# The states' products of a linear-attention layer: from two row groups and two PSUM banks to four of each

## The chip, the cores and the metric

One core of one Trainium2 chip runs the whole program. The metric is the device time of one execution in microseconds (us). The kernel before took 1279.37 us, the median of three runs (1279.18 to 1280.09).

## What is computed

The input is 8 sequences of 256 tokens with 256 features. They are normalised, and two branches read the result: an attention with 16 heads and 64 states to each head, and a feed-forward part with 4-bit weights (width 2048). Both are added to the input. The part that the change touches is `s` below and what is made of it.

```
xn = layernorm(x)
q, k = rope(xn @ Wq.T), rope(xn @ Wk.T)          # 16 heads of 128
v, g = xn @ Wv.T, xn @ Wg.T
s   = clip(xn @ Ws1.T @ Ws2.T + bs2, -32, 32)    # rank 16; 16 heads of 64 states
z   = cumlogsumexp(s, over the tokens)
es, enz = exp(s), exp(-z)
A   = tril(q @ k.T * scale)
ok  = enz * (A @ es)
qv  = softmax(ok, over the states)
W2  = tril((qv * enz) @ es.T)
o   = W2 @ v
o_g = o * rsqrt(mean(o * o) + 1e-5) * g_norm_weight * (g * sigmoid(g))
x + o_g @ Wo.T + ((gelu(xn @ Wg4.T) * (xn @ Wu4.T)) @ Wd4.T)
```

All arithmetic is in float32. The exponential of `s` is needed in two layouts: `es` with tokens on the partitions, `esT` with states on the partitions. `enz` is made from `esT` by a running sum along the tokens and a reciprocal.

## The kernel before

**Steps.** The 2048 tokens are cut into 4 groups of 512 (`G`, two sequences each), the 16 heads into 8 pairs. A step `n` is one group and one pair of heads, so there are 32 steps. Each works in three overlapping stretches: in the round of the main loop before its own the products of its states (`states`, L390) and of its rotated queries and keys (`rope`, L428); in its own round values and gates (`vg`, L482), scores (L500), logits (L517) and softmax (L540); in the next round the rest (`turn`, `weights`, `outputs`, `turn_back`, `close`). The feed-forward part (`ffn`, L344) is fed between them piece by piece, and so is the decoding of its 4-bit weights on VectorE (`decode_next`, L231).

**Order.** The order is fixed when the program is built. Tables (`POS`, `START`, `FEED`, L33 to L52) give every piece a place within its round; the main loop (L684) sorts them, calls each in turn, and after each call runs `tick` (L97). A piece issues its matmuls at once and leaves the work of the other engines behind as a chain (a Python generator); each `tick` issues one stage of every chain. So TensorE's instructions stand in the order of the pieces, and the other engines' in the order in which stages come up. On every engine the instructions then run in that order, and semaphores hold each back until its operands are there.

**Banks.** All products go to PSUM tiles of one bank (128 x 512 float32), from a pool of 8 (`bank`, L122). `new` (L103) makes a ninth user wait at build time: `need` (L92) ticks until the chains that read the eighth-last tile have been issued. On the chip, the first matmul into a bank waits for the last read of its former tenant.

**The low-rank input.** Once a group, `low_rank` (L373) multiplies the normalised tokens by `w_s1`. The 16 columns of `Ws1` stand twice among its 64 columns, at 0 and at 32, so the product `ps[0:64]` has the 16 values of each token on rows 0 to 15 and again on rows 32 to 47. ScalarE copies it to `rT` (L385) with a bias that is 1 on rows 16 and 48, so that the row of `bs2` in `w_s2` is added by the product itself. `w_s2` has the 17 rows at 0 and at 32 as well; it is loaded by four transfers on SyncE's queue (L167 to L169), after `w_s1` (L165) and `one_at` (L166) and ahead of the first attention weights (L170).

**The states.** In each call of `states`, 4 matmuls (L401) have a token block of `rT[0:17]` as the stationary operand and write `ps` (tokens on partitions), and 4 (L402) have the weights' 17 rows at 32 as the stationary operand and write `psT` (states on partitions). They alternate. VectorE then clamps both banks (L412, 512 elements each, `esT` first), ScalarE takes the exponentials (L415), VectorE the running sums (L420) and the reciprocals (L426).

**Around it.** In most rounds the logits (L526, read by L535), the weights of the step before (L596 and L600, read and masked by L497) and the states follow each other on TensorE, and then the transposes of the softmax (L547), which read the result of L535.

Of the kernel before, what the change touches and what calls it, by code (L numbers as in the profile page):

```python
# [10 lines left out]
F32 = mybir.dt.float32  # L11
I32 = mybir.dt.int32
AF = mybir.ActivationFunctionType
ALU = mybir.AluOpType
# [3 lines left out]
P = 128  # L18
B, T, D = 8, 256, 256
H, DK, M = 16, 128, 64  # L20
MLP = 2048
NTOK = B * T
G = 512
NG = NTOK // G
TC = G // P
EPS = 1e-5
CLAMP = 32.0
# [33 lines left out]
def layer_kernel(ctx: ExitStack, tc: tile.TileContext, a: dict, out: bass.AP):  # L61
# [15 lines left out]
    nc = tc.nc  # L77

    const = ctx.enter_context(tc.tile_pool(name="const", bufs=1))
# [5 lines left out]
    p1 = ctx.enter_context(tc.tile_pool(name="p1", bufs=1))  # L85
# [6 lines left out]
    def need(*gens):  # L92

        while any(c in chains for c in gens):
            tick()
# [7 lines left out]
    def new(pool, shape, tag, bufs=1, dtype=F32):  # L103

        users = held.setdefault(tag, [])
        if len(users) >= bufs:
            need(*users[-bufs])
        t = pool.tile(shape, dtype, tag=tag, name=tag, bufs=bufs)
        users.append([])
        at_tag[id(t)] = t, users[-1]  # L110
        return t
# [3 lines left out]
    def chain(gen, *tiles):  # L115

        chains.append(gen)
        for t in tiles:
            at_tag[id(t)][1].append(gen)
        return gen  # L120

    def bank():  # L122
        return new(ps_p, [P, 512], "ps", 8)
# [3 lines left out]
    xT = const.tile([P, 2, NTOK], F32, tag="xT", name="xT")  # L127
# [5 lines left out]
    cos = const.tile([P, T], F32, tag="cos", name="cos")  # L133
    sin = const.tile([P, T], F32, tag="sin", name="sin")

    w_s1 = const.tile([P, 2, 64], F32, tag="w_s1", name="w_s1")
    w_s2 = const.tile([64, H * M], F32, tag="w_s2", name="w_s2")
    one_at = const.tile([64, 1], F32, tag="one_at", name="one_at")
    gw = const.tile([P, 1], F32, tag="gw", name="gw")
    w_o = const.tile([P, H, D], F32, tag="w_o", name="w_o")  # L140
    w_gate = const.tile([P, 2, MLP], F32, tag="w_gate", name="w_gate")
# [14 lines left out]
    def load_w(n, k):  # L156

        if n < N:
            w = aw.tile([P, 2, 2, 2 * DK], F32, tag=f"wts{k}", name=f"wts{k}")
            nc.sync.dma_start(out=w, in_=a["wqkvg"][steps[n][1]][:, k : k + 2])  # L160
            wts[n, k] = w
# [2 lines left out]
    load_x(2, 2)  # L164
    nc.sync.dma_start(out=w_s1.rearrange("p c f -> p (c f)"), in_=a["ws1"])  # L165
    nc.sync.dma_start(out=one_at, in_=a["one_at"])  # L166
    for r in (0, 32):  # L167
        nc.sync.dma_start(out=w_s2[r : r + 16, :], in_=a["ws2"])
        nc.sync.dma_start(out=w_s2[r + 16 : r + 17, :], in_=a["bs2"])  # L169
    load_w(0, 0)  # L170
    nc.sync.dma_start(out=cos, in_=a["cos"])
    nc.sync.dma_start(out=sin, in_=a["sin"])
# [200 lines left out]
    def low_rank(g):  # L373

        need(*normed[g])
        rT = p1.tile([64, G], F32, tag="rT", name="rT")
        ps = bank()
        for c in range(2):
            nc.tensor.matmul(
                ps[0:64, :], lhsT=w_s1[:, c, :], rhs=xT[:, c, g * G : (g + 1) * G],  # L380
                start=c == 0, stop=c == 1,
            )

        def work():
            nc.scalar.activation(rT, ps[0:64, :], AF.Identity, bias=one_at)  # L385
            yield

        rTs[g] = rT, chain(work(), ps)

    def states(n):  # L390

        g, hp = steps[n]
        ms = slice(hp * P, (hp + 1) * P)
        (rT, c), to = rTs[g], of[n]
        need(c)
        es = to["es"] = new(p1, [P, TC, P], "es")
        esT = to["esT"] = new(p2, [P, G], "esT", 2)
        ps, psT = bank(), bank()
        for i in range(TC):
            ts = slice(i * P, (i + 1) * P)  # L400
            nc.tensor.matmul(ps[:, ts], lhsT=rT[0:17, ts], rhs=w_s2[0:17, ms], start=True, stop=True)  # L401
            nc.tensor.matmul(  # L402
                psT[:, ts], lhsT=w_s2[32:49, ms], rhs=rT[32:49, ts], start=True, stop=True
            )


        enz = to["enz"] = new(p2, [P, G], "enz", 2)

        def work():
            both = ((esT, psT), (es.rearrange("p i m -> p (i m)"), ps))  # L410
            for t, q in both:
                nc.vector.tensor_scalar(t, q, CLAMP, -CLAMP, ALU.min, ALU.max)  # L412
            yield
            for t, q in both:
                nc.scalar.activation(t, t, AF.Exp)  # L415
            yield
            for b in range(2):
                e = esT[:, b * T : (b + 1) * T]

                nc.vector.tensor_tensor_scan(  # L420
                    enz[:, b * T : (b + 1) * T], e, e, 0.0, ALU.add, ALU.max
                )
            yield
            for i in range(TC):
                r = enz[:, i * P : (i + 1) * P]
                nc.vector.reciprocal(r, r)  # L426
                yield

        to["states"] = chain(work(), ps, psT, es, esT, enz)

    def rope(n, j, which):

# [251 lines left out]
    for n in range(-1, N + 1):  # L684
        at = []
# [14 lines left out]
        if n == -1:  # L700
            put_norm(0, [0.0] * 4 + [0.1] * 2)
            put_at(0.2, low_rank, 0)
        if n + 1 < N:
            if n >= 0 and steps[n][1] == 7:
                put("low", 0, low_rank, steps[n][0] + 1)
            put("states", 0, states, n + 1)
            for k, (j, which) in enumerate(((0, 0), (0, 1), (1, 0), (1, 1))):
                put("rope", k, rope, n + 1, j, which)
            put("rope", 3, load_w, n + 2, 0)
# [45 lines left out]
def _tables():  # L755

    pos = np.arange(T, dtype=np.float32)
    inv = np.float32(1.0) / np.float32(10000.0) ** (
        np.arange(0, DK, 2, dtype=np.float32) / np.float32(DK)
    )  # L760
    ang = (pos[None, :] * inv[:, None].astype(np.float32)).astype(np.float32)
    c, s = np.cos(ang).astype(np.float32), np.sin(ang).astype(np.float32)
    return np.concatenate([c, c]), np.concatenate([-s, s])


def _layout(x):

    c = np.ascontiguousarray
    half = MLP // 2

    def pairs(ws):
        w = np.stack([w.T.reshape(P, 2, H // 2, 2 * DK) for w in ws])
        return c(w.transpose(3, 1, 0, 2, 4))

    def packed_in(w):
        return c(w.reshape(half, 2, -1).transpose(2, 1, 0).reshape(-1, MLP))

    def quarters(spread, of):
        ws = [packed_in(n[ff + w + of]).reshape(-1, 2, 4, 256) for w in ("gate", "up")]
        ws = [w.transpose(2, 0, 1, 3).reshape(4, -1, 512) for w in ws]  # L780
        w = n[ff + "down" + of]
        w = w.T.reshape(8, -1, D).transpose(1, 0, 2).reshape(-1, 4, 512)
        ws.append(w.transpose(1, 0, 2))
        return c(np.stack([[spread(w[q]) for w in ws] for q in range(4)]).reshape(12, P, 512))

    cos, sin = _tables()
    n = {k: np.asarray(v) for k, v in x.items()}
    at, ff = "L0_attn_", "L0_ffn_"
    return {
        "x": c(n[at + "hidden_states"].reshape(NTOK, D)),  # L790
        "wqkvg": pairs([n[at + w] for w in ("Wq", "Wk", "Wv", "Wg")]),
        "wo": c(n[at + "Wo"].T.reshape(H, DK, D).transpose(1, 0, 2)),
        "ws1": c(np.pad(n[at + "Ws1"].T.reshape(P, 2, 1, 16), [(0, 0)] * 3 + [(0, 16)]).repeat(2, 2).reshape(P, 128)),
        "one_at": (np.arange(64) % 32 == 16).astype(np.float32).reshape(64, 1),
        "ws2": c(n[at + "Ws2"].T),
        "bs2": c(n[at + "bs2"].reshape(1, H * M)),
        "gw": c(n[at + "g_norm_weight"].reshape(DK, 1)),
        "codes": quarters(lambda w: w, "_W_packed"),
        "scales": quarters(lambda w: w.repeat(16, 0), "_scales"),
        "cos": c(cos),  # L800
        "sin": c(sin),
    }
# [17 lines left out]
```

## Time and profile before

| | us |
|---|---|
| median of three runs | 1279.37 |
| the profiled execution, whole | 1279.47 |
| its span, first to last instruction | 1277.6 |
| L401 and L402, TensorE busy, each | 36.9 |
| L412 (`esT` and `es`), VectorE busy | 21.9 and 21.8 |
| L379, TensorE busy | 9.3 |
| L497, VectorE busy | 129.2 |

The profile is one execution. Engines are PE (TensorE's matmuls), PEld (TensorE's loads of the stationary operand), DVE (VectorE), ACT (ScalarE), POOL (GpSimd) and SP (SyncE, which issues the DMAs). A row of groups has the source line, the engine and the operation, tiles written and read, shapes, the number of records, then busy time in us and the mean of one in ns, then the idle time of the engine just before them. A matmul's shape "17*128" is 17 contracted rows by 128 columns of the stationary operand. A row of the timeline has start, duration (both us), engine, line, operation, tiles, shape, count, and in brackets how long the engine was idle before and what released it. The chain that ended last is followed back from the last instruction, at each step to what released it. Busy time counts overlapping records of one line once in some views and a group's mean is over single records, so the two need not multiply out.

### The profile page before, as it was taken

To read this page: it belongs to the slowest core of one execution; us is meant where nothing else is said; L and a number is where in the kernel's file an instruction comes from. 1 tells how busy PE (TensorE), PEld (TensorE's weight loads), DVE (VectorE), ACT (ScalarE), POOL (GpSimd) and SP (SyncE) were. 2 spreads that over 40 slices of the span, in tenths; PEclk is the share of its full clock that TensorE was granted. 3 is DMA by queue.
4 is the path that set the end of the run, shared out by engine and by line. 5 is a ranking of instruction groups with operands and counts; after the bars stand their busy time and mean duration, and the time that the engine had idled before them with its cause. 6 is when DMAs were issued, how large, how long until landed. Compare 5 with 4: busy or idle time off the path is not lost.

```text
span 1277.6 us, 17557 instructions
## 1 busy us (share of the span) xinstructions
PE 1262.4 (99%) x6448; PEld 914.2 (72%) x6448; DVE 817.4 (64%) x1592; ACT 531.9 (42%) x1677; POOL 441.9 (35%) x408
## 2 busy tenths in 40 slices
PE   7999999999999999999999999999999999999998
PEld 4577777776777777767677687777777767777776
DVE  6968756666656576664665766756665566566444
ACT  2444443453433454352444424445343345434232
POOL 4434333443223443232433413444332344322311
PEclk9999999999999999999999999999999999999999
DMA  4301111110111110011110010101001111101000
GB/s 162 116 17 50 34 33 50 34 49 2 50 34 34 50 33 18 17 34 50 50 34 17 31 38 33 34 33 34 1 33 34 34 33 32 36 17 43 25 17 17
DMA packets 18361, 47.73 MB, mean 37 GB/s; under 512 B 1986, under 2 KB 6466, under 8 KB 18276
## 3 DMA queue, kind: packets, MB, share of 16 engines
q1 hardware_dynamic: 18276, 46.61, 11.1%
q8 instruction: 51, 0.84, 0.3%
q14 instruction: 34, 0.28, 0.1%
HBM read 44.51 MB, written 2.10 MB: 36 GB/s over the span
## 4 chain that ended last, share of the span: by engine, by line
PE 94%; DVE 4%; ACT 1%; issue 1%; POOL 0%; DMA 0%; POOLq 0%; DVEq 0%; ACTq 0%
PE ps L489 16%; PE ps L437 16%; PE ps L669 9%; PE ps L338 8%; PE ps L318 8%; PE ps L298 8%; PE ps L507 4%; PE ps L526 4%; PE ps L596 3%; PE ps L401 2%; PE ps L621 2%; PE ps L618 2%; PE ps L617 2%; PE ps L510 2%; PE ps L651 2%; PE ps L547 1%
## 5 line engine op out<-in xcount | busy, mean ns | idle before, releaser
L450 POOL TENSOR_TENSOR z<-z,sin 128x512 f32<-128x512 f32 x128 | 163.3, 1276 | 448.8 <-ACT z L447 448.5
L437 PE MATMUL ps<-xT,wts 128*128 128x512 f32 x512 | 240.9, 593 | 0.0
L489 PE MATMUL ps<-wts,xT 128*128 128x256 f32 x1024 | 239.7, 379 | 0.0
L489 PEld LDWEIGHTS ps<-wts,xT 128*128 128x128 f32 x1024 | 191.9, 190 | 55.8 <-issue 30.8
L437 PEld LDWEIGHTS ps<-xT,wts 128*128 128x128 f32 x512 | 94.3, 191 | 85.1 <-issue 79.3
L497 DVE TENSOR_TENSOR at<-ps,mask 128x384 f32<-128x384 f32 x256 | 129.2, 551 | 21.6 <-PE ps L510 9.4
L306 POOL TENSOR_SCALAR t<-t 128x512 f32<-128x512 f32 x64 | 40.1, 627 | 267.0 <-ACT t L304 265.0
L446 ACT COPY z<-ps 64x512 f32<-64x512 f32 x128 | 74.6, 583 | 135.9 <-PE ps L437 117.5
L415 ACT ACTIVATE esT<-esT 128x512 f32<-128x512 f32 x32 | 20.2, 630 | 252.4 <-DVE esT L412 252.4
L298 PE MATMUL ps<-xT,w_gate 128*128 128x512 f32 x256 | 120.7, 594 | 0.0
L318 PE MATMUL ps<-xT,w_up 128*128 128x512 f32 x256 | 120.6, 593 | 0.0
L277 DVE TENSOR_TENSOR res<-ps,res 128x512 f32<-128x512 f32 x64 | 44.1, 689 | 119.5 <-PE ps L338 59.8
L338 PE MATMUL ps<-w_down,inter 128*128 128x256 f32 x512 | 116.0, 380 | 0.9 <-DVE inter L326 0.9
L426 DVE RECIPROCAL enz<-enz 128x128 f32<-128x128 f32 x128 | 116.8, 932 | 0.0
L669 PE MATMUL ps<-w_o,ogT 128*128 128x256 f32 x512 | 115.6, 379 | 0.0
L338 PEld LDWEIGHTS ps<-w_down,inter 128*128 128x128 f32 x512 | 95.9, 190 | 14.4 <-DVE inter L326 1.7
L669 PEld LDWEIGHTS ps<-w_o,ogT 128*128 128x128 f32 x512 | 95.6, 190 | 14.6 <-issue 2.2
L448 DVE TENSOR_TENSOR k<-ps,cos 128x512 f32<-128x512 f32 x64 | 44.0, 687 | 87.2 <-ACT z L447 87.1
L451 POOL TENSOR_TENSOR q<-q,z 128x512 f32<-128x512 f32 x64 | 81.6, 1275 | 21.7 <-DVE q L448 13.9
L451 POOL TENSOR_TENSOR k<-k,z 128x512 f32<-128x512 f32 x64 | 81.5, 1273 | 9.0 <-DVE k L448 4.3
L448 DVE TENSOR_TENSOR q<-ps,cos 128x512 f32<-128x512 f32 x64 | 44.0, 688 | 63.0 <-ACT z L447 62.7
L559 ACT ACTIVATE pr<-ps,mx 128x64 f32<-128x64 f32 x256 | 76.5, 325 | 12.9 <-DVE mx L556 12.3
(81 smaller groups left out, 2119.5 us busy)
## 6 DMA issues: line engine op xcount, KB each, us to landing
wts<-in_wqkvg_dram SPq DMA_DIRECT2D x64, 512.0 KB, 3.6
pk<-in_codes_dram SPq DMA_DIRECT2D x12, 256.0 KB, 4.5
sc<-in_scales_dram SPq DMA_DIRECT2D x12, 256.0 KB, 4.7
w_o<-in_wo_dram SPq DMA_DIRECT2D x4, 512.0 KB, 6.0
out_dram<-res SPq DMA_DIRECT2D x8, 256.0 KB, 2.1
res<-in_x_dram SPq DMA_DIRECT2D x3, 512.0 KB, 5.4
res<-in_x_dram SPq DMA_DIRECT2D x2, 256.0 KB, 2.8
w_s<-in_ws_dram SPq DMA_DIRECT2D x3, 64.0 KB, 2.4
```

The lines of the kernel that those rows point to most:

```text
L298: nc.tensor.matmul(pg, lhsT=w_gate[:, c, ns], rhs=xT[:, c, gs], start=c == 0, stop=c == 1)
L318: nc.tensor.matmul(pu, lhsT=w_up[:, c, ns], rhs=xT[:, c, gs], start=c == 0, stop=c == 1)
L338: nc.tensor.matmul(ps[:, k, :], lhsT=inter[g, n][0][:, (i + k) * P : (i + k + 1) * P], rhs=w_dn[:, n, :], start=n == 2 * q, stop=n == 2 * ...
L426: nc.vector.reciprocal(r, r)
L437: nc.tensor.matmul(ps, lhsT=w[:, c, :], rhs=xT[:, c, g * G : (g + 1) * G], start=c == 0, stop=c == 1)
L448: nc.vector.tensor_tensor(y, pv, cos_b, ALU.mult)
L450: nc.gpsimd.tensor_tensor(z, z, sin_b, ALU.mult)
L451: nc.gpsimd.tensor_tensor(y, y, z, ALU.add)
L489: nc.tensor.matmul(ps[:, k, :], lhsT=xT[:, c, tt], rhs=w[:, which, c, :], start=c == 0, stop=c == 1,)
L497: nc.vector.tensor_tensor(t, ps[:, 0 : 3 * P], mask, ALU.mult)
L559: nc.scalar.activation(pr[:, k, :], pv[:, k, :], AF.Exp, bias=mx[:, k : k + 1], scale=SCALE, accum_out=sm[:, k : k + 1],)
L669: nc.tensor.matmul(ps[:, k, :], lhsT=ogT[hh][0][:, (i + k) * P : (i + k + 1) * P], rhs=w_o[:, (hp // 2) * 4 + hh, :], start=hh == 0, stop= ...
```

## The change

The 17 rows of the low-rank input and of the weights are held four times, at rows 0, 32, 64 and 96. The 8 matmuls of a call of `states` go to four banks: row groups 0 and 1 make the token layout, token blocks 0 and 1 in the first bank and 2 and 3 in the second; row groups 2 and 3 make the state layout in the same way. The four row groups follow each other in the program, and each comes up twice. The clamp reads half a bank at a time, so there are four of 256 elements in place of two of 512. `ws2` and `bs2` come as one array, so each copy is one transfer.

```diff
-    w_s1 = const.tile([P, 2, 64], F32, tag="w_s1", name="w_s1")
-    w_s2 = const.tile([64, H * M], F32, tag="w_s2", name="w_s2")
-    one_at = const.tile([64, 1], F32, tag="one_at", name="one_at")
+    w_s1 = const.tile([P, 2, P], F32, tag="w_s1", name="w_s1")
+    w_s2 = const.tile([P, H * M], F32, tag="w_s2", name="w_s2")
+    one_at = const.tile([P, 1], F32, tag="one_at", name="one_at")
...
-    for r in (0, 32):
-        nc.sync.dma_start(out=w_s2[r : r + 16, :], in_=a["ws2"])
-        nc.sync.dma_start(out=w_s2[r + 16 : r + 17, :], in_=a["bs2"])
+    for r in range(0, P, 32):
+        nc.sync.dma_start(out=w_s2[r : r + 17, :], in_=a["ws2"])
...
-        rT = p1.tile([64, G], F32, tag="rT", name="rT")
+        rT = p1.tile([P, G], F32, tag="rT", name="rT")
...
-                ps[0:64, :], lhsT=w_s1[:, c, :], rhs=xT[:, c, g * G : (g + 1) * G],
+                ps, lhsT=w_s1[:, c, :], rhs=xT[:, c, g * G : (g + 1) * G],
...
-            nc.scalar.activation(rT, ps[0:64, :], AF.Identity, bias=one_at)
+            nc.scalar.activation(rT, ps, AF.Identity, bias=one_at)
...
-        ps, psT = bank(), bank()
-        for i in range(TC):
-            ts = slice(i * P, (i + 1) * P)
-            nc.tensor.matmul(ps[:, ts], lhsT=rT[0:17, ts], rhs=w_s2[0:17, ms], start=True, stop=True)
-            nc.tensor.matmul(
-                psT[:, ts], lhsT=w_s2[32:49, ms], rhs=rT[32:49, ts], start=True, stop=True
-            )
+        pss = [bank() for _ in range(4)]
+        for i in range(2):
+            for r, ps in enumerate(pss):
+                rows = slice(32 * r, 32 * r + 17)
+                k = 2 * (r % 2) + i
+                tok, st = rT[rows, k * P : (k + 1) * P], w_s2[rows, ms]
+                lhsT, rhs = (tok, st) if r < 2 else (st, tok)
+                nc.tensor.matmul(
+                    ps[:, i * P : (i + 1) * P], lhsT=lhsT, rhs=rhs, start=True, stop=True
+                )
...
-            both = ((esT, psT), (es.rearrange("p i m -> p (i m)"), ps))
-            for t, q in both:
-                nc.vector.tensor_scalar(t, q, CLAMP, -CLAMP, ALU.min, ALU.max)
+            both = (esT, es.rearrange("p i m -> p (i m)"))
+            for t, r in ((both[0], 2), (both[1], 0)):
+                for k in range(2):
+                    nc.vector.tensor_scalar(
+                        t[:, k * T : (k + 1) * T], pss[r + k][:, 0:T], CLAMP, -CLAMP,
+                        ALU.min, ALU.max,
+                    )
             yield
-            for t, q in both:
+            for t in both:
                 nc.scalar.activation(t, t, AF.Exp)
...
-        to["states"] = chain(work(), ps, psT, es, esT, enz)
+        to["states"] = chain(work(), *pss, es, esT, enz)
```

The host's layout follows: `ws1` repeats its padded columns four times (256 values a row in place of 128), `one_at` has 128 rows, and `ws2` has `bs2` as its 17th row.

More of the change, by code (lines that the diff above doesn't have):

```diff
@@ L792, in _layout @@
         "wo": c(n[at + "Wo"].T.reshape(H, DK, D).transpose(1, 0, 2)),
[L793 to L796, printed above, removed]
+        "ws1": c(np.pad(n[at + "Ws1"].T.reshape(P, 2, 1, 16), [(0, 0)] * 3 + [(0, 16)]).repeat(4, 2).reshape(P, 256)),
+        "one_at": (np.arange(P) % 32 == 16).astype(np.float32).reshape(P, 1),
+        "ws2": c(np.concatenate([n[at + "Ws2"].T, n[at + "bs2"].reshape(1, H * M)])),
         "gw": c(n[at + "g_norm_weight"].reshape(DK, 1)),
```

## The prediction

> **What bounds the kernel now.** I read the page first: busy shares, then the chain that ended last.
>
> ```profile
> span 1277.6 us, 17557 instructions
> PE 1262.4 (99%) x6448; PEld 914.2 (72%) x6448; DVE 817.4 (64%) x1592; ACT 531.9 (42%) x1677; POOL 441.9 (35%) x408
> PE 94%; DVE 4%; ACT 1%; issue 1%; POOL 0%; DMA 0%; POOLq 0%; DVEq 0%; ACTq 0%
> ```
>
> The chain is 94% matmul, and between the first and the last of the forty slices PE is never under nine tenths. A matmul can be modelled as busy while it is not at its peak, so next I took the groups by line with shapes kept apart, for the two lines that the change replaces and for the clamp that reads their banks:
>
> ```profile
> L402 PE MATMUL ps<-rT,w_s 17*128 17x128 f32 x256 | 36.9, 283 | 0.0
> L401 PE MATMUL ps<-w_s,rT 17*128 17x128 f32 x256 | 36.9, 283 | 0.0
> L412 DVE TENSOR_SCALAR esT<-ps 128x512 f32<-128x512 f32 x32 | 21.9, 684 | 0.0
> ```
>
> Each line has 4 matmuls in each of 32 calls, so 128, and 256 records: a float32 matmul is recorded as two passes. The durations overlap, so they don't say how long a block takes. The timeline of PE does; this is the block of one step:
>
> ```profile
> 336.37 0.49 PE L600 MATMUL ps<-prT,esT 64*128 64x128 f32 x4
> 336.79 0.37 PE L401 MATMUL ps<-w_s,rT 17*128 17x128 f32 x1
> 336.79 0.37 PE L402 MATMUL ps<-rT,w_s 17*128 17x128 f32 x1
> 337.00 0.27 PE L401 MATMUL ps<-w_s,rT 17*128 17x128 f32 x1
> 337.01 0.27 PE L402 MATMUL ps<-rT,w_s 17*128 17x128 f32 x1
> 337.11 0.27 PE L401 MATMUL ps<-w_s,rT 17*128 17x128 f32 x1
> 337.12 0.27 PE L402 MATMUL ps<-rT,w_s 17*128 17x128 f32 x1
> ...
> 337.67 0.27 PE L401 MATMUL ps<-w_s,rT 17*128 17x128 f32 x1
> 337.68 0.27 PE L402 MATMUL ps<-rT,w_s 17*128 17x128 f32 x1
> 337.88 0.66 PE L547 MATMUL ps<-ident,ok 128*128 128x128 f32 x4
> ```
>
> See that L401 (rows 0 to 16) and L402 (rows 32 to 48) already start together, 0.007 us apart: two row groups run at once. Eight such rounds follow each other; from the second start (337.00) to the eighth (337.67) are six intervals, 0.67 / 6 = 0.111 us each. See also that the second pass of a matmul does not hold back the first pass of the next one in the other row group, though it stands before it in the program. The chain of waits, followed through this block, is the block's passes alone and then L547, so its length is on the path.
>
> Last, who waits on whom: all of PE's own waits sum to 11.4 us, 8.3 of them at L205, and the weight-load waits apart from "issue" to some 31 us, mostly start-up or hidden. There is little slack to fall into, and little waiting to lose.
>
> **What the Trainium skill says.** "TensorE: Matmul & The Clock Gate", Part 3 (packing small matmuls), says that matmuls on different 32-row groups run concurrently, some 4 ns apart, and gives a measured 3.07x for four row groups at 512 columns. The trace agrees for two groups (0.007 us apart, 0.111 us a round, the same as L510's lone 128-column pass: 0.22 us for two); four at once no line here shows. "TensorEngine Tiling (Array Packing)", Gotcha 1, says that row tiles must write different PSUM banks and that row tiling raises the pressure on PSUM; before, L401 and L402 do write two banks. For the smaller clamp, "VectorE: DVE Perf Modes", section on the TRN2 errata, gives (N+151)/0.96 ns: 691 at N=512, where L412 shows 684.
>
> **The change part by part.** Sums are against the profiled execution, 1279.47 us (span 1277.6 and 1.9 around it), 0.1 above the median.
>
> 1. The states' matmuls. Before: 8 matmuls in two groups, 16 passes, 8 rounds. After: the same 8 on four groups, 4 rounds. Removed: 4 x 0.111 = 0.444 us; added: a stagger of 3 x 0.007 instead of 1 x 0.007, 0.014. So 0.43 us a call. The gaps at both ends of the block (L600 to L401, and 337.68 to L547) stay: the shape of the array changes there as before. Is it on the path? Of 32 calls, 30 are. The first two (18.8 and 46.9 us) lie where the chain runs over DVE (15.2 to 15.7 of each 16 us busy between 16 and 64 us) and PE waits; there the gain is nothing. 30 x 0.43 = 12.9 us off. Bounds: 0 if four groups run no denser than two, 13.8 with all 32.
>
> 2. Banks. Two more of eight banks are taken in each call. PE's order of instructions is the same otherwise, DVE's has about twenty small moves, none near a states block. I took the built programs' bank of each tile and, on the times of before, the time from a bank's last read to its next first matmul. Before, the smallest is 0.36 us. In the new plan, in 27 calls the last bank is the one whose logits DVE has read (L535) only 0.8 us earlier; it just holds, as PE can start 0.05 us after DVE ends (L326 ends at 65.12, L338 starts at 65.17); I take 0.06. L547, after the block, mostly gets a bank of the weights' masking (L497), with 0.8 us or more to spare, of which 0.43 are used up. Three calls do not hold. One is shown here:
>
> ```profile
> 220.16 0.66 PE L547 MATMUL ps<-ident,ok 128*128 128x128 f32 x4
> 220.25 1.01 DVE L497 TENSOR_TENSOR at<-ps,mask 128x384 f32<-128x384 f32 x2
> ```
>
> L547 would come at 220.16 - 0.43 = 219.73, but its bank is read by the first L497 until 220.25 + 0.55 = 220.80 (DVE is behind, with decoding in front of the masks): wait 1.07 + 0.06 = 1.13. The same at 791.05, where the mask starts at 791.25: 1.24. At 561.6 the block's own fourth bank is 0.26 short: 0.32. Together 2.7 us on. Bounds: 0 if DVE comes earlier there, 6 if the calls with 0.4 left fail by 0.3 each as well.
>
> 3. The clamps. Two of 512 elements become four of 256. By the page's formula one takes 424 ns, by L412's 684 less 256 x 1.04 it is 418; summed, 0.30 us more a call. But DVE overlaps neighbours: the two L412 start at 338.00 and 338.60, 0.60 apart, and four L497 of 384 elements take 1.95 us, so (1.95 - 0.55) / 3 = 0.467 apart. The line through both, 1.04 ns an element, puts 256 at 0.334 apart: 4 x 0.334 - 2 x 0.60 = 0.13 us a call. DVE idles 36% of the span, so 30 calls hide it: behind the clamps stand the softmax's maximum (L555) and the scans (L420), which PE needs (L576, L596) most of a step later. In the first two calls DVE is the path: 0.3 us on (0.26 to 0.6). If the cover were gone everywhere, 0.13 to 0.30 x 32 = 4 to 10 us.
>
> 4. Low rank. L379 has 128 columns of weights instead of 64 in 8 matmuls; the moving side stays 512 columns. Its weight load goes from 137 ns to some 190 (L437's), mostly beside the running pass: 0.2 us in all, bounds 0 and 0.8 (16 passes x 53 ns). L385 has 128 partitions instead of 64 and the same 512 elements: nothing.
>
> 5. Loads. Six issues stay six on SP. The bytes go from 200 to 400 KB ahead of the first weights; at the 300 to 400 GB/s of that stretch 0.6 us. The first L437 starts at 13.01, well after its weights, and the first decode (L250, 10.70) is followed by four idle us of DVE: nothing. If uncovered, 0.6.
>
> Sum: -12.9 + 2.7 + 0.3 + 0.2 = -9.7; 1279.5 - 9.7 = 1269.8 us.
>
> **The rivals.**
> - A, partly denser: four groups start together, but a round takes longer, say 0.16 us (midway to 0.222). Per call 0.888 - 0.64 - 0.014 = 0.234, 30 calls 7.0, less 2.3 for banks (shorter shift) and 0.5: 1275.3. For it: nobody in this trace runs four groups, and 3.07 is not 4. Against: going from one group to two costs nothing.
> - B, slower: weight loads. Each pass has its own load of 128 columns, 187 ns of record at a spacing of 0.111; two fit at once. If the path from SBUF is full with two, a round of four takes 2 x 0.111 + 0.014 = 0.236: 30 x (4 x 0.236 - 0.888) = +1.7, banks 1.8, parts 3 and 4 0.5: 1283.5. It decides from a round of about 0.20 us. For it: the page's figure is at 512 columns, where loads weigh less. Against: no price for the second group.
> - C, DVE lags: all 0.30 us of a call land on PE through banks, 9.6 us: 1279.5 - 12.9 + 2.7 + 9.6 + 0.2 = 1279.1. For it: DVE is 3.96 of 4 us busy in 337 to 341. Against: PE hardly waits on DVE, and the masks stand ahead of the clamps.
> - D, the change doesn't do what it says: matmuls issue strictly in order with both passes, so two groups are the most that ever overlap; no gain, about 1281.8. Against: the first round above already starts the second matmul before the first one's second pass.
>
> **How the numbers follow.** Forecast 0.73, A 0.11, B 0.07, C 0.05, D 0.04. Predicted 1269.8. The forecast's own range, with the bounds of parts 1 to 4, is 1265.5 to 1273.5; A reaches 1275 to 1277, so 1265.5 to 1276.5 holds about 8 in 10. A difference of 0.2% (2.6 us) is what a measurement here can tell. Faster: forecast and most of A, 0.84. Slower: B and a part of D, 0.09. Same 0.07.
>
> **What would show it.** In the timeline of a block: four starts within 0.02 us, and four rounds 0.111 apart; PE's busy time down by some 13 us, L547 0.43 us sooner. New PE waits of L547 on L497 near 220 and 790. The new clamp at about 0.42 us, DVE's sum up by 9 us of overlapping records. It is wrong if rounds are 0.2 apart, if PE waits at many blocks for L535 or L497, or if DVE takes a larger share of the chain.

## The result, and the profile after

The changed kernel took 1279.01 us (median of 14 runs, 1277.62 to 1279.72), the kernel before 1279.54 beside it (14 runs, 1279.02 to 1280.32). The ratio is 0.9994, with a 95% interval of 0.9986 to 1.0002: no difference that can be told. Among the 14 runs, seven with a mean granted clock of TensorE of 0.996 took 1278.92 to 1279.72 us and five with 1.000 took 1277.62 to 1278.49, so some 0.8 us of the median goes with the lower clock. The profiled execution took 1279.42 us. Its page:

```profile
span 1277.6 us, 17625 instructions
PE 1253.4 (98%) x6448; PEld 903.9 (71%) x6448; DVE 821.3 (64%) x1656; ACT 532.0 (42%) x1677; POOL 441.7 (35%) x408
PE 91%; DVE 5%; DMA 1%; issue 1%; POOL 1%; ACT 0%; SPq 0%; POOLq 0%; DVEq 0%; ACTq 0%
```

The span is the same to a tenth of a us, but PE is busy 9.0 us less, and the chain that ended last has 1% of DMA and some SPq in it that it did not have. So the matmuls did get shorter, and something else took the time. First the block of one step, in PE's timeline:

```profile
344.65 0.38 PE L405 MATMUL ps<-w_s,rT 17*128 17x128 f32 x2
344.66 0.38 PE L405 MATMUL ps<-rT,w_s 17*128 17x128 f32 x2
344.86 0.28 PE L405 MATMUL ps<-w_s,rT 17*128 17x128 f32 x2
344.88 0.28 PE L405 MATMUL ps<-rT,w_s 17*128 17x128 f32 x2
344.97 0.28 PE L405 MATMUL ps<-w_s,rT 17*128 17x128 f32 x2
344.99 0.28 PE L405 MATMUL ps<-rT,w_s 17*128 17x128 f32 x2
345.08 0.28 PE L405 MATMUL ps<-w_s,rT 17*128 17x128 f32 x2
345.10 0.28 PE L405 MATMUL ps<-rT,w_s 17*128 17x128 f32 x2
345.31 0.66 PE L553 MATMUL ps<-ident,ok 128*128 128x128 f32 x4
```

Each line is two passes, so four start within 0.02 us, and there are four rounds 0.11 us apart. From the first start to the last a block takes 0.457 us in 30 of the 32 calls (0.69 and 0.75 in the two at 227 and 567); before it was 0.89 in every one.

Where the time went shows when the start of the same instruction is taken from both timelines, here the first softmax transpose of a step (L547 before, L553 after):

| before, us | after, us | after less before |
|---|---|---|
| 51.5 | 59.2 | +7.66 |
| 71.7 | 80.2 | +8.53 |
| 183.0 | 190.8 | +7.76 |
| 220.2 | 228.6 | +8.46 |
| 562.7 | 567.8 | +5.13 |
| 753.8 | 757.0 | +3.16 |
| 791.0 | 795.0 | +3.97 |
| 1169.9 | 1169.8 | -0.09 |

Nearly every step after 72 us gains 0.43 us, and three lose (144, 220 and 791). But all of them start from 8 us behind: the start-up lost what the 29 blocks after it then won back. In the timeline of the start, the low-rank product (L378), the first rotated queries (L443) and SyncE's issues:

```profile
9.53 3.78 PE L378 MATMUL ps<-xT,w_s 128*128 128x512 f32 x4 [0.68 <-ACT xT L210]
19.78 7.70 PE L443 MATMUL ps<-xT,wts 128*128 128x512 f32 x12 [6.47 <-DMA wts<-in_wqkvg_dram]
...
2.69 1.26 SPq L168 DMA_DIRECT2D w_s<-in_ws_dram  x4
4.00 0.36 SPq L160 DMA_DIRECT2D wts<-in_wqkvg_dram  x1
4.40 0.43 SPq L170 DMA_DIRECT2D cos<-in_cos_dram  x1
5.40 0.33 SPq L171 DMA_DIRECT2D sin<-in_sin_dram  x1
5.78 1.77 SPq L226 DMA_DIRECT2D pk<-in_codes_dram  x1
9.93 0.33 SPq L227 DMA_DIRECT2D sc<-in_scales_dram  x1
12.76 0.33 SPq L226 DMA_DIRECT2D pk<-in_codes_dram  x1
15.75 0.33 SPq L227 DMA_DIRECT2D sc<-in_scales_dram  x1
```

The first rotated queries (L443; L437 before, at 13.01) wait for their weights until 19.78, though these were issued at 4.00, earlier than before (4.47). Right after the four loads of `w_s2` SyncE issues normally, and then only one transfer every three us. Its waits name the transfers that hold it:

```profile
SPq L227 <- DMA w_s<-in_ws_dram: 5.0, 2, 2.6
SPq L226 <- DMA w_s<-in_ws_dram: 2.5, 1, 2.5
SPq L160 <- DMA w_s<-in_ws_dram: 2.5, 1, 2.5
```

These waits are the program's own: by the trace its loads use eight semaphores in turn, and each waits until the load that stands eight before it in the queue has landed, here a copy of `w_s2`. In the kernel before the same waits were over before they began. The first weights are not held by this, since they were issued ahead of it. The DMA view of the first 32 us, in 40 slices, says how fast bytes moved (after, then before):

```profile
GB/s 0 0 88 337 280 94 118 215 296 242 215 236 51 82 271 26 26 113 241 26 44 210 126 26 110 323 254 243 312 128 31 13 0 0 0 0 0 0 0 0
```

```profile
GB/s 0 0 78 364 264 155 77 169 253 294 320 312 346 379 399 415 399 259 33 0 0 0 0 0 0 0 0 0 0 0 51 292 243 224 355 393 81 0 164 164
```

Before, the rate climbs to 415 GB/s. After, it falls to 26 in four slices between 12 and 19.2 us. A view of the first two of them has the mean busy share of the 16 DMA engines and the GB/s as its last two figures:

```profile
12.00:13.60 1.60, 1.31 (x2) 0.00 (x0) 0.00 (x0) 0.25 (x1) 0.00 (x0) 1.00 0.07 26
```

A share of 0.07 is about one engine in 16, and at 26 GB/s that engine moves a packet of 4 KB in 0.16 us. A row of `w_s2` is one such packet, four transfers of 17 rows are 68, and 68 x 0.16 = 10.9 us; 17 of them are 2.7. The semaphore updates in the trace say the same. A transfer of 16 rows in the kernel before has 16 of them as its parts land. A transfer of 17 rows has two, one right at its issue and one when all has landed, and the four land at 9.91, 12.74, 15.74 and 18.54 us. Of the first weights' 16 updates, 15 have come by 8.83 us, and the last comes at 19.73; before, all 16 had come by 8.94. So the four loads went through one engine, one after the other, and the weights' share on that engine stood behind them.

The wait is not all of the loss. The first products after it ran at half pace, as the starts of L443's weight loads show:

```profile
23.35 0.34 PEld L443 LDWEIGHTS ps<-xT,wts 128*128 128x128 f32 x1 [0.52 <-issue]
24.20 0.30 PEld L443 LDWEIGHTS ps<-xT,wts 128*128 128x128 f32 x1 [0.52 <-issue]
24.74 0.19 PEld L443 LDWEIGHTS ps<-xT,wts 128*128 128x128 f32 x1 [0.24 <-issue]
25.17 0.19 PEld L443 LDWEIGHTS ps<-xT,wts 128*128 128x128 f32 x1 [0.24 <-issue]
```

Up to 24.20 they are 0.85 us apart, from 24.74 on 0.43. In the kernel before the pace of 0.43 begins at 14.00, and fewer products lie ahead of it. The wait costs 6.5 us, the slow products 1.8. In this execution the granted clock is also 0.50 from 68.8 to 72.2 us, which costs some 0.9. Why the clock is lower in these places was not tested.

### The profile page after: what moved, and what is told of

Same layout as the page of the kernel before. It is cut to its first block, busy times and chain, and to the rows that moved or that the text cites. A ratio compares the mean times of both kernels' runs of the same rounds, so it can differ in the third digit from the quotient of the medians.

```text
span 1277.6 us, 17625 instructions
## 1 busy us (share of the span) xinstructions
PE 1253.4 (98%) x6448; PEld 903.9 (71%) x6448; DVE 821.3 (64%) x1656; ACT 532.0 (42%) x1677; POOL 441.7 (35%) x408
## 4 chain that ended last, share of the span: by engine, by line
PE 91%; DVE 5%; DMA 1%; issue 1%; POOL 1%; ACT 0%; SPq 0%; POOLq 0%; DVEq 0%; ACTq 0%
PE ps L495 16%; PE ps L443 16%; PE ps L675 9%; PE ps L337 9%; PE ps L317 8%; PE ps L297 8%; PE ps L513 4%; PE ps L532 4%; PE ps L602 3%; PE ps L516 2%; PE ps L627 2%; PE ps L624 2%; PE ps L623 2%; PE ps L657 2%; PE ps L405 1%; PE ps L553 1%
## 5 line engine op out<-in xcount | busy, mean ns | idle before, releaser
L443 PE MATMUL ps<-xT,wts 128*128 128x512 f32 x512 | 242.7, 597 | 6.5 <-DMA wts<-in_wqkvg_dram 6.5
L443 PEld LDWEIGHTS ps<-xT,wts 128*128 128x128 f32 x512 | 95.0, 192 | 92.6 <-issue 79.5
L640 POOL TENSOR_TENSOR ss<-ss,nhalf 128x4 f32<-128x4 f32 x64 | 64.8, 1014 | 60.6 <-DVE ss L639 58.9
L644 DVE SCALAR_TENSOR_TENSOR og<-ps,ss,sgate 128x128 f32<-128x128 f32 x256 | 70.6, 340 | 19.2 <-POOL ss L640 19.2
```

What stands on the lines that cost most here:

```text
L443: nc.tensor.matmul(ps, lhsT=w[:, c, :], rhs=xT[:, c, g * G : (g + 1) * G], start=c == 0, stop=c == 1)
L644: nc.vector.scalar_tensor_tensor(og[:, i, :], po[:, i, :], ss[:, i : i + 1], sg[:, i, j * DK : (j + 1) * DK], ALU.mult, ALU.mult,)
```

## The experiments

The theory at this point: the block gains what was forecast, a few banks take back some 3 us, and the shape of the load, 17 rows, costs 8 us at the start. The rivals: the 200 KB more are to blame, or the number of issues; or something in the four-group block or its banks at the start.

### The loads

**Split.** Each copy is loaded as 16 rows and 1, as before the change.

```diff
-        nc.sync.dma_start(out=w_s2[r : r + 17, :], in_=a["ws2"])
+        nc.sync.dma_start(out=w_s2[r : r + 16, :], in_=a["ws2"][0:16, :])
+        nc.sync.dma_start(out=w_s2[r + 16 : r + 17, :], in_=a["ws2"][16:17, :])
```

> The changed kernel, with each copy of w_s2 loaded as a transfer of 16 rows and one of 1 row, as before the change, in place of one of 17 rows: eight transfers, the same bytes. Theory S (a 17-row transfer goes through a single DMA engine, so 68 rows of 4 KB queue there one after the other at 0.16 us each, some 11 us, and the first attention weights wait behind them): the start-up delay of 7.7 us at the first L553 goes, the steps keep their 0.43 us each, about 1270.5 us (1269.5 to 1271.5). Rival B (the 200 KB more are what delays the weights): the first L443 still waits for its weights and the time stays within 1.5 us of 1279. Rival I (the number of issues on SP counts): four more issues of 0.3 us each, slower than 1279.

Measured: 1270.88 us, ratio 0.9931 (0.9916 to 0.9945). The first L444, which is L443 here, starts at 12.94. The same bytes and four issues more: neither of those was the cause.

**One padded transfer.** The array has 15 zero rows after each 17 and is loaded by one transfer of 128 rows.

```diff
-    for r in range(0, P, 32):
-        nc.sync.dma_start(out=w_s2[r : r + 17, :], in_=a["ws2"])
+    nc.sync.dma_start(out=w_s2, in_=a["ws2"])
...
```

> The changed kernel, with w_s2 loaded by one transfer of 128 rows from an array padded with zero rows to 32 a group: 512 KB in place of 272, one issue in place of four. Theory S: all 16 DMA engines share it, 8 rows each; start-up as in the kernel before but for some 1 us of bytes, about 1270.5 us (1269.5 to 1272). Rival B (bytes): 240 KB more than the changed kernel, so slower than 1279.

Measured: 1270.34 us, ratio 0.9926 (0.9909 to 0.9942), with 240 KB more than the changed kernel. Bytes are out.

**The load alone.** The kernel before, with the four 17-row loads into a tile of 128 rows, of which it uses the lower two copies.

```diff
-    w_s2 = const.tile([64, H * M], F32, tag="w_s2", name="w_s2")
+    w_s2 = const.tile([P, H * M], F32, tag="w_s2", name="w_s2")
...
-    for r in (0, 32):
-        nc.sync.dma_start(out=w_s2[r : r + 16, :], in_=a["ws2"])
-        nc.sync.dma_start(out=w_s2[r + 16 : r + 17, :], in_=a["bs2"])
+    for r in range(0, P, 32):
+        nc.sync.dma_start(out=w_s2[r : r + 17, :], in_=a["ws2"])
...
```

> The kernel before with the changed kernel's four 17-row loads of w_s2 and nothing else of the change (the two upper copies are not used). Theory S: the start-up delay alone, 1279.5 + 8 = 1287.5 us (1286 to 1289), with the first L437 waiting for its weights until about 19.5 us. Rival (the delay comes from the four-group block or the four banks at the start, not from the load): 1279.5 within 1 us.

Measured: 1286.56 us, ratio 1.0055 (1.0040 to 1.0070), 0.9 us under the 1287.5 expected, inside its range and clear of the rival. From its list of PE's waits, where L436 is L437 of before:

```profile
PE ps L436 <- DMA wts<-in_wqkvg_dram: 6.1, 1, 6.1
```

Against the kernel before, the first softmax transpose comes 7.69 us late, and every later step between 7.63 and 7.67. So the load costs its time once, at the start, and nothing afterwards.

**The load moved back.** The 17-row loads stand after the first weights, tables and packed weights.

```diff
-    for r in range(0, P, 32):
-        nc.sync.dma_start(out=w_s2[r : r + 17, :], in_=a["ws2"])
     load_w(0, 0)
...
     load_packed(2)
+    for r in range(0, P, 32):
+        nc.sync.dma_start(out=w_s2[r : r + 17, :], in_=a["ws2"])
```

> The changed kernel with the same four 17-row loads, issued after the first attention weights, cos, sin and the first packed weights instead of ahead of them. Theory S: what queues behind is then only the second group's traffic; the first L443 starts near 13 us as before, but the states need w_s2 at about 19 us and it lands 11 us after its issue at some 10 us, so a wait of a few us at the first states block, partly hidden since PE waits there anyway: 1271 to 1275 us. Rival B: as e1, no change from 1279 is expected from order alone if bytes decide, since the same bytes come before the states.

Measured: 1274.85 us, ratio 0.9961 (0.9946 to 0.9976). The weights come in time (L441 starts at 13.29), and now the first states wait for `w_s2` itself, as expected. From PE's timeline:

```profile
18.62 0.94 PE L403 MATMUL ps<-w_s,rT 17*128 17x128 f32 x4
21.84 0.46 PE L403 MATMUL ps<-rT,w_s 17*128 17x128 f32 x2 [2.28 <-DMA w_s<-in_ws_dram]
24.50 0.55 PE L403 MATMUL ps<-rT,w_s 17*128 17x128 f32 x1 [2.20 <-DMA w_s<-in_ws_dram]
```

The two passes of each of the first two groups' first matmul are the first line; the third group's copy has landed at 21.84, the fourth's at 24.50, 2.66 us later. 17 rows at 0.16 us are 2.7: the copies land one after the other, at the pace of one engine.

**18 rows.** Is it that 17 is more than 16, or that 17 has no divisor? One zero row more tells.

```diff
-        nc.sync.dma_start(out=w_s2[r : r + 17, :], in_=a["ws2"])
+        nc.sync.dma_start(out=w_s2[r : r + 18, :], in_=a["ws2"])
...
```

> The changed kernel with each of the four loads of w_s2 having 18 rows (one of zeros) in place of 17, so 4 KB more a transfer. Theory D (the transfer is divided over the largest number of DMA engines up to 16 that divides its rows: 17 gives 1, 18 gives 9): no queue of 68 rows on one engine, the first weights come in time, 1270.6 us (1269.5 to 1271.6). Rival (any transfer of more than 16 rows that isn't a multiple of 16 is kept on one engine): as the changed kernel, 1279 to 1280.

Measured: 1270.33 us, ratio 0.9929 (0.9912 to 0.9945). One row more makes the kernel some 9 us faster than 17 rows. The first L443 starts at 13.13, and the rate never falls to 26 before the loads of the start have landed:

```profile
GB/s 0 0 90 353 291 189 195 220 189 255 273 288 334 407 410 430 392 382 95 3 0 0 0 0 0 0 0 0 0 5 205 329 243 349 403 104 0 0 69 259
```

This is what the Trainium skill says in "DMA: Bandwidth & Descriptors", in the section on why a DMA increments its semaphore by 16: a transfer from SyncE's queue is divided over the largest number of engines up to 16 that divides the sizes of the outer dimension on both sides, and 127 partitions, for instance, go to a single one. The runs agree for 17 rows (26 GB/s, one engine) and for 18: by the page's rule they go to 9 engines, and in the trace each 18-row transfer has ten semaphore updates, one right at its issue and nine as its parts land, between 4.64 and 5.83 us for the first.

### The banks and the clamps

**Four banks, two groups.** The kernel before, with four banks and four clamps, but matmuls in the two groups at rows 0 and 32, and its own loads.

```diff
-        ps, psT = bank(), bank()
+        pss = [bank() for _ in range(4)]
...
+            for r in (0, 2, 1, 3):
+                ps = pss[r]
+                row = 32 * (r // 2)
+                rows = slice(row, row + 17)
...
```

> The kernel before with four banks and four clamps of 256 elements in the states, but its matmuls still in the two row groups at rows 0 and 32 and its own loads. Theory (gain from the groups, price from the banks): blocks stay 0.89 us from first to last start, waits of L547 for masks near 220 (0.7) and 791 (0.8), 0.3 at 562, and some 0.3 to 0.8 at the start from the clamps: 1281.5 us (1280.8 to 1282.5). Rival (part of the gain came from writing to more banks): shorter blocks and a time under 1279.5.

Measured: 1281.34 us, ratio 1.0013 (1.0006 to 1.0019): slower by 1.5 to 1.7 us. A block still takes 0.89 to 0.98 us from first to last start. Against the timeline of before, L547's counterpart loses 0.69 us at 220, 0.09 at 563 and 0.81 at 791, and nowhere else moves by more than 0.12. Its waits name the banks that the masks read (L505 is L497, L555 is L547):

```profile
PE ps L555 <- DVE at L505: 1.3, 2, 0.7
```

So four banks with four clamps cost about 1.7 us, the next run puts the clamps at nothing, and the gain belongs to the row groups alone.

**Half clamps.** The kernel before with each clamp cut in two.

```diff
             for t, q in both:
-                nc.vector.tensor_scalar(t, q, CLAMP, -CLAMP, ALU.min, ALU.max)
+                for k in range(2):
+                    kt = slice(k * T, (k + 1) * T)
+                    nc.vector.tensor_scalar(t[:, kt], q[:, kt], CLAMP, -CLAMP, ALU.min, ALU.max)
```

> The kernel before with each clamp cut into two of 256 elements, nothing else. Theory: DVE carries 0.13 us more a step, hidden outside the start: 1279.5 + 0.3 (0 to 0.8). Rival C of the prediction (DVE's extra work lands on PE): up to 1289, 0.3 us in every step.

Measured: 1279.56 us, ratio 0.9998 (0.9989 to 1.0007). DVE's extra work does not reach the end. In the changed kernel the source line's view gives the new clamp:

```profile
L415 DVE TENSOR_SCALAR esT<-ps x64: 406/411/415, 30.7 to 1170.7; 128x256 f32<-128x256 f32 x64
```

The three figures are the shortest, median and longest in ns.

**Decoding later.** The wait near 220 in the changed kernel looks like this in its timeline, at 228:

```profile
227.41 0.69 DVE L254 SCALAR_TENSOR_TENSOR w_gate<-u,sc 128x512 f32<-128x512 f32 x1
228.01 1.02 DVE L503 TENSOR_TENSOR at<-ps,mask 128x384 f32<-128x384 f32 x2
228.62 0.66 PE L553 MATMUL ps<-ident,ok 128*128 128x128 f32 x4 [0.82 <-DVE at L503]
```

L553 starts 0.06 us after the first of the two masks has ended (228.01 + 0.55), and the masks stand behind a piece of decoding (L254). If the queue of DVE makes the wait, it goes when the decoding stands elsewhere. From the padded kernel, in the two rounds with two pieces:

```diff
-            put_at((k - sent + 0.3) / (upto - sent), lambda k=k: k < len(parts) or decode_next())
+            put_at((k - sent + (0.6 if n in (5, 20) else 0.3)) / (upto - sent), lambda k=k: k < len(parts) or decode_next())
```

> The kernel of the padded load (e2), with the two pieces of weight decoding in rounds 5 and 20, the only later rounds with two, put 0.15 of a round later: after the states instead of ahead of them on VectorE. Theory: L552's waits for L502 near 220 and 787 us (1.1 and 1.2 us) come from the decoding that stands ahead of the masks on DVE while the extra banks make L552 need a mask's bank; with it moved both waits go, 1270.3 - 2.4 = 1268.0 us (1267.3 to 1268.8). Rival (eight banks are simply too few there): the waits stay and the time stays at 1270.3 within 0.6.

Measured: 1268.75 us, ratio 0.9914 (0.9900 to 0.9929). By the timelines about half of it came, 1.3 of 2.4 us: the wait near 787 is gone, but the one near 218 has moved to the next product.

```profile
217.47 0.42 DVE L189 BATCH_NORM_STATS2 st<-res 128x6 f32<-128x256 f32 x1
...
218.75 0.68 DVE L310 SCALAR_TENSOR_TENSOR t<-t,ps 128x512 f32<-128x512 f32 x1
...
219.48 3.72 PE L674 MATMUL ps<-w_o,ogT 128*128 128x256 f32 x16 [0.98 <-DVE t L310]
```

L674 needs the bank that L310 reads, and L310 now stands behind the statistics of a normalisation (L189 to L191). Those can move too:

```diff
-            put_norm(gn, NORM_AT)
+            put_norm(gn, (0.3, 0.33) + NORM_AT[2:] if n == 5 else NORM_AT)
```

> The kernel of e5 with the first two pieces of the last group's normalisation in round 5 moved behind the states as well (0.3 and 0.33 of the round in place of 0.2 and 0.293). Theory: in e5 the wait near 218 us only moved from L552 to L674, which gets the bank that L310 reads, with the statistics (L189, 1.3 us) ahead of L310 on DVE; with them behind it too the wait of 1.0 us goes: 1268.75 - 1.1 = 1267.7 us (1267.0 to 1268.4). Rival (the bank is short whatever stands on DVE): no change from e5, 1268.3 to 1269.5.

Measured: 1267.79 us, ratio 0.9908 (0.9893 to 0.9922), the fastest of the study. Against the kernel of the experiment before it, L674 comes 1.14 us earlier, and the next pass of L674 0.10; nothing else moves. So these banks were late because of what stood ahead of their readers on DVE, and both waits went when that was moved.

## Why the prediction was wrong

**The step that failed is part 5, the loads.** It counted six issues as six and 200 KB more at the rate of the stretch, and so 0 us, 0.6 if uncovered. It took in the size of a transfer and not its shape: 17 rows in one transfer in place of 16 and 1. The 17 rows went through one engine, and the first weights' share on that engine waited behind them until 19.73 us. It cost 7.7 us at the first softmax transpose, and 7.1 us of the whole in the kernel with the loads alone (1286.56 - 1279.50). Neither the forecast nor any rival had it, and the lower and upper ends were both drawn without it. The trace of before shows 16 updates for a 16-row transfer and two for a 1-row one, but has no 17-row transfer; the page named above states the rule, and part 5 did not apply it.

The forecast was 9.7 us of gain, and 0.5 was measured. Of the 9.2 between them the loads are 7.1, the lower clock of half the runs some 0.8, and the low rank and a third block, both below, 0.5 each. Rival C's figure, 1279.1, is the measured time almost exactly, and that is chance: what it names, VectorE holding PE back by 0.3 us in every step, is not there.

With the loads mended, 1270.88, 1270.34 and 1270.33 us were measured, against 1269.8 forecast. The other parts:

- Part 1, the groups: 0.43 us a call was forecast, 0.433 is measured (0.89 - 0.457). The spacing of a round stayed 0.11 us with four groups; rivals A and B (0.16 and more) and D are out. The first two blocks gain almost nothing in the end, as forecast: in the split kernel what follows each comes 0.43 us earlier, and the next waits for DVE (L533 for L504 at 45.46 on the timeline of before, L205 for the normalisation at 59.39) give back 0.38 and 0.39. A third, at 105, gives back 0.55 at the next normalisation (L205 at 131), which was not forecast.
- Part 2, the banks: 1.13, 1.24 and 0.32 us were forecast in three places, and nothing in the others. The same three are there. Compared with a step that gains 0.43, they lose 1.12 and 1.24, each with 0.07 more at the product behind, and 0.30: 2.8 us in place of 2.7. Reading the bank plan against the times of before told this to a tenth of a us.
- Part 3, the clamps: some 0.42 us was forecast for one, 411 ns is measured. The 0.3 us at the start is not seen in the kernel with half clamps alone. Rival C is out.
- Part 4, the low rank: 0.2 us was forecast, with 0.8 as the upper bound. In each of the last three groups L378's first pass comes 0.10 us later after L532, and its second 0.10 later after the first; at the start it is 0.11 once: 0.7 in all. The later passes keep their 0.43 us, so there the wider weight load is hidden, as part 4 had it; the loss is where the product begins. L532 has 64 columns of weights, as L379 had and L378 has not; whether this change of shape is the reason was not tested.

So in the changed kernel 29 blocks after the start win 29 x 0.433 = 12.6 us, banks give back 2.8, low rank 0.6 and the normalisation 0.5; that leaves 8.7, and the start had lost 8.5 by the step at 72 us (the wait, the slow products and the stretch at half clock, less what the first blocks had won).

## What to carry to other kernels

A DMA has a shape as well as a size: where an edit merges or re-cuts transfers, count the rows and ask over how many engines they divide, above all ahead of the first weights: here one late share of 16 held back a whole load. The products of 17 rows and 128 columns ran side by side in the four row groups of TensorE at the pace of two, 0.11 us a round. What they take is banks, and the three places where that hurt were found before the run, from the bank plan and the times of the last reads.

## What was not expected of the hardware

- A transfer of 17 rows of 4 KB runs at 26 GB/s, a row in 0.16 us, where its neighbours run at up to 415. One row more, 18, spreads over nine engines and removes the delay.
- A late load costs PE more than the wait: with the 17-row loads in front the pace of 0.43 us for a 512-column pass begins only after 24.2 us, in place of 14.0, and up to there it is 0.85.
- With four groups the starts in a round are still about 0.007 us apart. But a matmul that waits for data holds back those behind it, in whatever group: with the late load the first two groups' second matmuls, whose rows had landed, ran only after the fourth group's first (24.50).
